# Loading the edge indices of a graph kernel: order of the first loads, and how the edge pairs are stored

## The chip, the cores and the metric

The kernel runs on one core of a Trainium2 chip. The metric is the device time of one execution in microseconds; several executions are timed and their median is given. The profile is of one further execution, with its own time. Engines are called TensorE (PE in the profile; PEld is its weight load), VectorE (DVE), ScalarE (ACT), GpSimd (POOL) and SyncE (SP). SyncE, ScalarE and GpSimd each issue DMA transfers from a queue of their own; in the profile q1 holds SyncE's transfers, q10 ScalarE's and q0 GpSimd's.

## What is computed

There are 6250 nodes with 64 features and 206,250 directed edges, sorted by their destination `dst`; each node has a self-loop among them. Four graph layers follow one another, each on the layer norm of its input and each added to it:

```python
edge_index = jnp.stack([src, dst])
h = relu(layernorm(x)); x = x + L0(h, edge_index, W3, b3, W4, b4)
h = relu(layernorm(x)); x = x + L1(h, edge_index)
h = relu(layernorm(x)); x = x + L2(h, edge_attr_64, src, dst, ...)
h = relu(layernorm(x)); x = x + L3(edge_index, h)
```

L0 is two normalised graph convolutions with a linear map behind each. L1 is one normalised sum over neighbours. L2 puts every edge's attributes through a small MLP, gates the gathered source node with the result, and takes the root of the mean of squares over each node's edges. L3 is three normalised sums over neighbours, averaged with its input. All but L2 are products of the same 6250 by 6250 matrix of edge counts with node features.

## The kernel before

Nodes are padded to 6272, in 49 blocks (`NB`) of 128 (`P`). The kernel builds the matrix of edge counts once, in 8-bit floats, and keeps it in DRAM as `A`. It multiplies with it in every layer but L2. `fast` is the path that runs; `general` follows only if the edges break an assumption of `fast`.

The part that the change touches is the very beginning of `fast`, which prepares the matrix:

- X, the node features, is loaded by ScalarE's queue (L752). `dst` is loaded as `dst_i` by SyncE (L762) and `src` as `src_i` by ScalarE (L764). Both are 128 rows of `K1` = 1616 indices, 206,848 (`EP`) with padding.
- `look` (L767) is every 101st `dst`, times 49. It is stored to DRAM as `looks` (L770), and later read back onto all partitions as `near`, 128 rows of 2048 numbers (L800).
- VectorE makes of every edge a pair of floats, `dst * 49 + (src >> 7)` and `src & 127` (L772 to L777), and SyncE stores these 128 rows of 12,928 bytes to DRAM as `pairs` (L778). Then one row `none`, filled with a large number, is stored over everything from edge 206,250 (`E`) on (L781). The tail of the pair store and this filler cover the same places.
- For 25 columns (`GC`) of 128 two-node groups, VectorE compares `near` with each group's first key and counts (L804), which gives `begin_i`, the approximate position of each group's edges (L807 to L809, in three pieces). The pools that follow (`rpool`, `opool`, `wpool`) reuse the memory of the index tiles and of `near`.
- GpSimd gathers `near2`, 101 pairs from that position on (L872; the profile calls it `near`), VectorE counts again for the exact position, and GpSimd gathers `run`, 128 pairs from there (L881). This happens 25 times each. The gathers read `pairs` as a whole tensor, so they come after every store into it.
- From the runs, `key` is made through TensorE's transposes. `build` compares it with running numbers, which gives one-hot tiles `lo` and `hd` (L852), and their product is 32 columns of counts (L861). ScalarE writes them to a `strip` of 448 columns (L865). SyncE stores each of the 14 strips to `A` (L997).
- The node degrees come from the keys of all runs, over `degs` and `by_block` (L921, L924). They are needed for the normalised features `U3`, with which the first convolution starts (L748).

The layer norm of X (L694 to L703, in 7 groups) and the turning of W3 and W4 (loads L822 and L824, TensorE L833 and L836, copies L834 and L837) also lie in this stretch.

The order of instructions on each engine is the planner's. It works from the program's order and from times that it assumes, except in blocks that are marked as ordered by hand; the beginning is not marked. [...] A tile's memory is given out again when the accesses to it are finished.

Of the kernel before, what the change touches and what calls it, by code (L numbers as in the profile page):

```python
# [8 lines left out]
F32 = mybir.dt.float32  # L9
BF16 = mybir.dt.bfloat16  # L10
FP16 = mybir.dt.float16
I32 = mybir.dt.int32
AF = mybir.ActivationFunctionType
OP = mybir.AluOpType
AX = mybir.AxisListType

P = 128
N = 6250
D = 64
NB = 49  # L20
# [4 lines left out]
E = 206250  # L25
J = 8
G = -(-E // (P * J))
EP = G * P * J
# [556 lines left out]
K1 = EP // P  # L585
LOOK = 101
NS = K1 // LOOK * P
# [29 lines left out]
def fast(ctx, tc, bad, x, src, dst, edge_attr, W3, b3, W4, b4, w1, b1, w2, b2, Bw, Bb, Cw, Cb,  # L617
         pAw, pAb, pBw, pBb, out):

    nc = tc.nc  # L620
# [11 lines left out]
    pairs = dram.tile([EP + 512, 2], F32, name="pairs")  # L632
    looks = dram.tile([NS], F32, name="looks")
# [115 lines left out]
                             start=(i < 2), stop=(i >= 3 * n - 2))  # L749

    X = node.tile([P, NB, D], F32, name="X")
    nc.scalar.dma_start(X, x.rearrange("(b p) f -> p b f", p=P))  # L752
    apart = ctx.enter_context(ExitStack())
    early = ExitStack()
    early_pool = early.enter_context(tc.tile_pool(name="early_pool", bufs=1, reuse_waits="tile"))
    with ExitStack() as ph:

        ipool = ph.enter_context(tc.tile_pool(name="ipool", bufs=1, reuse_waits="tile"))
        with ExitStack() as first:
            dpool = first.enter_context(tc.tile_pool(name="dpool", bufs=1, reuse_waits="tile"))  # L760
            dst_i = dpool.tile([P, K1], I32, name="dst_i")
            nc.sync.dma_start(dst_i, dst.rearrange("(p k) -> p k", p=P))  # L762
            src_i = dpool.tile([P, K1], I32, name="src_i")
            nc.scalar.dma_start(src_i, src.rearrange("(p k) -> p k", p=P))  # L764

            look = dpool.tile([P, NS // P], F32, name="look")
            nc.vector.tensor_scalar(  # L767
                look, dst_i.rearrange("p (i l) -> p i l", l=LOOK)[:, :, 0], float(NB), None,
                op0=OP.mult)
            nc.sync.dma_start(looks.rearrange("(p i) -> p i", p=P), look)  # L770
            hi = dpool.tile([P, K1], I32, name="hi")
            nc.vector.tensor_scalar(hi, src_i, 7, None, op0=OP.logical_shift_right)  # L772
            nc.vector.tensor_scalar(src_i, src_i, P - 1, None, op0=OP.bitwise_and)
            pair = dpool.tile([P, K1, 2], F32, name="pair")
            nc.vector.scalar_tensor_tensor(pair[:, :, 0], dst_i, float(NB), hi,
                                           op0=OP.mult, op1=OP.add)
            nc.vector.tensor_copy(pair[:, :, 1], src_i)  # L777
            nc.sync.dma_start(pairs[:EP, :].rearrange("(p k) t -> p k t", p=P), pair)  # L778
            none = dpool.tile([1, 2 * (EP + 512 - E)], F32, name="none")
            nc.vector.memset(none, float(2 ** 22))  # L780
            nc.sync.dma_start(pairs[E:, :].rearrange("(o e) t -> o (e t)", o=1), none)  # L781

        start_of = ipool.tile([P, GC], F32, name="start_of")
        nc.gpsimd.iota(start_of, pattern=[[2 * NB * P, GC]], base=0, channel_multiplier=2 * NB,
# [9 lines left out]
        begin_i = ipool.tile([P, GC], I32, name="begin_i")  # L794
        exact_i = ipool.tile([P, GC], I32, name="exact_i")
        junk = ipool.tile([P, P], F32, name="junk")
        looked = ExitStack()
        npool = looked.enter_context(tc.tile_pool(name="npool", bufs=1, reuse_waits="tile"))
        near = npool.tile([P, NS], F32, name="near")
        nc.sync.dma_start(near, looks.partition_broadcast(P))  # L800
        for c0, c1 in ((0, 3), (3, 10), (10, GC)):
            for c in range(c0, c1):
                w = min(max(int(c * 2 * P * E / N / LOOK) - 22, 0), NS - SW)
# [4 lines left out]
                                    op0=OP.mult, op1=OP.max)  # L808
# [21 lines left out]
        with ExitStack() as ps:  # L830
            psum = ps.enter_context(tc.tile_pool(name="ps0", bufs=1, space=PSUM, reuse_waits="tile"))
            p = psum.tile([P, SG, P], F32, name="p_a", bufs=2)
            nc.tensor.transpose(p[:D, 0, :], W3_sb, ident)  # L833
            nc.vector.tensor_copy(W3T, p[:D, 0, :])  # L834
            p = psum.tile([P, SG, P], F32, name="p_a", bufs=2)
# [34 lines left out]
            for c in range(GC):  # L870
# [6 lines left out]
                                        op0=OP.is_lt, op1=OP.add, accum_out=n)  # L877
                nc.vector.tensor_add(exact_i[:, c:c + 1], begin[:, c:c + 1], n)
            for c in range(GC):
# [6 lines left out]
                                        op0=OP.subtract)  # L886
                nc.scalar.activation(digits[:, 1, :], run[:, :, 1], AF.Copy)
                p = psum.tile([P, 1024], BF16, name="p_dig")
# [6 lines left out]
                if c % 9 == 8 or c == GC - 1:  # L895
                    c0 = c // 9 * 9
                    p = psum.tile([P, 512], F32, name="p_node")
# [19 lines left out]
            p = psum.tile([P, 512], F32, name="p_node")  # L917
# [7 lines left out]
            p = psum.tile([P, 512], F32, name="p_node")  # L925
# [571 lines left out]
    with ExitStack() as ph:  # L1497
# [5 lines left out]
        for layer in range(3):  # L1503
# [25 lines left out]
            else:  # L1529
                for s in range(CS):  # L1530
                    if s % 2 == 0:
                        whole = apool.tile([P, CB, W], COUNT, name="piece")
                        nc.sync.dma_start(whole, A[s // 2][:, blocks(NC - 1), :])
                    t = whole[:, :, s % 2 * CW:(s % 2 + 1) * CW]
                    p = psum.tile([P, 512], F32, name="p_sum", bufs=2)
# [9 lines left out]
def gnn_kernel(tc, *args):  # L1545
    nc = tc.nc
    with tc.tile_pool(name="verdict", bufs=1) as verdict:
        bad = verdict.tile([1, 1], I32, name="bad")
        fast(tc, bad, *args)
        n = nc.values_load(bad[0:1, 0:1], min_val=0, max_val=2 ** 30)  # L1550
        with tc.If(n > 0):
            general(tc, *args)
# [31 lines left out]
```

## Time and profile before

| | us |
|---|---|
| median of 3 runs | 3608.37 (3608.08 to 3612.73) |
| profiled execution, its own time | 3611.97 |
| its span, first to last instruction | 3610.2 |
| first indirect gather of `pairs` (L872) | starts 48.11 |
| first convolution (L748) | starts 156.9 |
| first product with `A` from DRAM (L1026) | starts 579.0 |
| gathers of the edge layer (L1354) | 1041.9 to 3125.3 |
| last matmul (L1026) | starts 3601.5 |

Over the span TensorE is busy 84%, VectorE 54%, GpSimd 46% and ScalarE 34%; the mean granted TensorE clock is 0.904. Times in the profile run from the span's start. A line of a timeline gives start, length, engine, line, operation, output and input, and in brackets the engine's idle time before it and what ended that. A DMA-issuing instruction is shown on its queue (SPq, ACTq) with the time of the issue; the transfer itself comes later. The DMA view counts packets for each queue[...].

### The profile page before, as it was taken

Reading aid. Unit: us, or ns where it says so; the run is one execution under the profiler, and the core shown is the slowest. Engines: PE = TensorE matmul, PEld = TensorE weight load, DVE = VectorE, ACT = ScalarE, POOL = GpSimd, SP = SyncE. Lnnn points to the kernel's source line nnn. Section 1 sums busy time; section 2 is a strip of 40 time slices with the busy share of each in tenths; the row PEclk is TensorE's granted clock in tenths of the full one; section 3 lists DMA queues with packets and bytes.
Section 4 is the critical chain, followed back from the end, with each engine's and each line's share of the span. In section 5 each row is a group of like instructions: output and inputs, shape, how many; then the busy total and the mean of one; then the engine's idle time right before and its main releaser. Section 6 shows DMA issues by size and latency. Waiting matters only on the chain.

```text
span 3610.2 us, 59581 instructions
## 1 busy us (share of the span) xinstructions
PE 3039.4 (84%) x24393; PEld 2141.2 (59%) x24393; DVE 1954.2 (54%) x3899; ACT 1239.3 (34%) x2024; POOL 1665.0 (46%) x1889
## 2 busy tenths in 40 slices
PE   1699999999977777878878887878887888799999
PEld 0466667999954444444444444444454444489998
DVE  6899993532235546556555655655655565531111
ACT  1577772000023434434333443434433444210000
POOL 4200001000037777777777777777777777400000
PEclk9699999999988888889889888888988888799999
DMA  3233335565532223223323232322332322256664
GB/s 107 64 91 95 95 95 189 188 205 183 178 101 80 77 53 84 71 70 97 86 68 97 70 85 79 88 68 76 91 88 70 94 70 68 81 166 194 196 206 143
DMA packets 229312, 388.76 MB, mean 108 GB/s; under 512 B 137573, under 2 KB 139743, under 8 KB 228771
## 3 DMA queue, kind: packets, MB, share of 16 engines
q1 hardware_dynamic: 170420, 321.51, 28.3%
q0 software_dynamic: 55104, 60.65, 8.3%
q8 instruction: 193, 3.16, 0.4%
q10 hardware_dynamic: 3504, 2.70, 0.3%
q14 instruction: 91, 0.75, 0.1%
HBM read 340.47 MB, written 44.24 MB: 107 GB/s over the span
## 4 chain that ended last, share of the span: by engine, by line
POOL 35%; PE 35%; issue 14%; DMA 9%; DVE 5%; ACT 1%; POOLq 0%; DVEq 0%; SPq 0%; ACTq 0%
POOL v L1354 35%; PE p_acc L1026 21%; PE p_sum L748 7%; DMA v<-Vp_dram,src_g 7%; PE p_a L861 4%; DMA near<-pairs,begin_i 1%; PE p_node L739 1%; DMA piece<-A 1%; DVE lo L852 0%; DMA run<-pairs,exact_i 0%; PE p_acc L1023 0%; PE p_node L970 0%; PE p_bc L1380 0%; DMA X<-in_x 0%; PE p_node L975 0%
## 5 line engine op out<-in xcount | busy, mean ns | idle before, releaser
L1354 POOL DMA_INDIRECT v<-Vp_dram,src_g x1616 | 1592.1, 985 | 859.9 <-issue 828.6
L1026 PE MATMUL p_acc<-U,piece 128*128 128x192 bf16 x9604 | 817.7, 246 | 5.0 <-DMA piece<-A 5.0
L1026 PEld LDWEIGHTS <-piece 128*128 128x128 fp8e4 x9604 | 798.9, 98 | 17.0 <-DMA piece<-A 5.2
L1380 PE MATMUL p_bc<-BC,h 128*128 128x256 f32 x1616 | 585.8, 496 | 0.0
L1389 DVE TENSOR_TENSOR m<-gate,v 128x512 f32<-128x512 f32 x202 | 140.3, 694 | 762.5 <-DMA v<-Vp_dram,src_g 627.7
L1380 PEld LDWEIGHTS p_bc<-BC,h 128*128 128x128 f32 x1616 | 341.2, 234 | 154.7 <-issue 116.2
L1396 ACT ACTIVATE m<-m 128x512 bf16<-128x512 f32 x202 | 127.2, 630 | 821.9 <-DVE m L1391 821.9
L748 PEld LDWEIGHTS <-U 128*64 128x64 bf16 x4116 | 231.1, 112 | 215.4 <-issue 68.3
L1036 DVE TENSOR_REDUCE zg<-p_acc 128x128 f32<-128x384 f32 x112 | 56.3, 507 | 537.4 <-PE p_acc L1026 536.9
L865 ACT ACTIVATE strip<-p_a 128x784 fp8e4<-128x784 f32 x392 | 302.3, 820 | 112.6 <-PE p_a L861 112.0
L1376 PE MATMUL p_bc<-BC_b,ones 3*128 3x512 bf16 x404 | 180.9, 448 | 167.3 <-DVE m L1390 167.2
L1260 PE MATMUL p_sum<-ident_b,piece 128*128 128x128 bf16 x1372 | 154.9, 238 | 183.7 <-DVE junk L1266 183.4
L1260 PEld LDWEIGHTS <-piece 128*128 128x128 fp8e4 x1372 | 117.7, 107 | 318.8 <-issue 301.2
L1376 PEld LDWEIGHTS <-ones 3*128 3x128 bf16 x404 | 37.5, 93 | 439.4 <-DVE m L1390 235.3
L1366 PE MATMUL p<-h,w_d 128*128 128x512 f32 x404 | 253.5, 713 | 38.6 <-ACT h L1370 38.6
L748 PE MATMUL p_sum<-piece,U 128*64 128x448 fp8e4 x2058 | 238.1, 374 | 27.0 <-DVE junk L1266 18.7
L1370 ACT ACTIVATE h<-p,b_c 128x512 f32<-128x512 f32 x404 | 255.8, 684 | 12.9 <-PE p L1366 12.6
L1266 DVE SCALAR_TENSOR_TENSOR junk<-p_sum,there 128x512 bf16<-128x512 f32 (+1 forms) x392 | 242.1, 618 | 27.3 <-PE p_sum L1260 18.7
L748 PE MATMUL p_sum<-strip,U 128*64 128x448 fp8e4 x2058 | 242.0, 359 | 2.5 <-ACT U L711 1.4
L852 DVE TENSOR_TENSOR lo<-count,key 128x2048 bf16<-128x2048 bf16 x196 | 239.6, 1222 | 0.0
L861 PEld LDWEIGHTS <-lo 128*128 128x128 bf16 x3136 | 164.7, 103 | 98.6 <-DVE lo L852 75.8
L861 PE MATMUL p_a<-hd,lo 128*128 128x98 bf16 x3136 | 195.1, 217 | 32.6 <-DVE lo L852 31.1
(198 smaller groups left out, 3308.5 us busy)
## 6 DMA issues: line engine op xcount, KB each, us to landing
piece<-A SPq DMA_DIRECT2D x249, 784.0 KB, 4.3
e<-in_edge_attr SPq DMA_DIRECT2D x202, 256.0 KB, 2.7
A<-strip SPq DMA_DIRECT2D x14, 2744.0 KB, 13.1
v<-Vp_dram,src_g POOLq DMA_INDIRECT x1616
there<-A SPq DMA_DIRECT2D x28, 784.0 KB
pairs<-pair SPq DMA_DIRECT2D x1, 1616.0 KB, 5.3
Vp_dram<-v SPq DMA_DIRECT2D x7, 224.0 KB
out<-X SPq DMA_DIRECT2D x6, 224.0 KB
```

Of the source, the lines that this page charges most:

```text
L748: nc.tensor.matmul(p[half * D:(half + 1) * D, :w], U3[:, b, k, :], at_block, start=(i < 2), stop=(i >= 3 * n - 2))
L852: nc.vector.tensor_tensor(t, of.unsqueeze(1).to_broadcast(t.shape), key[:, k, at:at + GB].rearrange("p (h j) -> p h j", j=GQ) .unsqueeze(2 ...
L861: nc.tensor.matmul(p[:, j, :2 * NB], lo[:, g // GQ, :, g % GQ], hd[:, g // GQ, :, g % GQ], start=True, stop=True)
L865: nc.scalar.activation(strips[s][:, :, col:col + 2 * SG].rearrange("p b (j l) -> p b j l", l=2), p[:, :, :2 * NB].rearrange("p j (b l) -> ...
L1026: nc.tensor.matmul(p[d // 2][:, d % 2 * 3 * D:(d % 2 + 1) * 3 * D], t[:, b, d * P:(d + 1) * P], U3[:, k * CB + b, :, :].rearrange("p t f - ...
L1260: nc.tensor.matmul(p[:, a - a0, :], held["here", i, k][:, a, b * P:(b + 1) * P], ident_b, start=True, stop=True)
L1266: nc.vector.scalar_tensor_tensor(junk[:, :(a1 - a0) * P], p[:, :a1 - a0, :].rearrange("p a q -> p (a q)"), 15.5, of_there, op0=OP.min, op1 ...
L1354: nc.gpsimd.indirect_dma_start(out=v[:, j, :], out_offset=None, in_=Vp_dram[:, :], in_offset=bass.IndirectOffsetOnAxis(ap=src_g[:, g, j:j ...
L1366: nc.tensor.matmul(of[g][p], w, of[g].pop(x), start=True, stop=True)
L1370: nc.scalar.activation(of[g][t], of[g].pop(p), **how)
L1376: nc.tensor.matmul(p_bc[:, 4 * b:4 * b + 4].rearrange("p j o f -> p (j o f)"), ones, BC_b, start=True, stop=False)
L1380: nc.tensor.matmul(p_bc[:, 2 * q:2 * q + 2].rearrange("p j o f -> p (j o f)"), h2[:, q * P:(q + 1) * P], BC, start=False, stop=(k == 1))
```

## The change

- `src_i` is loaded by SyncE behind `dst_i`.
- `near` gets its memory before the index tiles, in a stack that is closed after the comparisons, and is read directly behind the store of `looks`. The index tiles stay allocated as long.
- X's load is traced behind these, still on ScalarE's queue.
- `none` is filled at the start.
- The pair store is cut in two: `whole` = E // K1 = 127 rows, and of the last row the pairs that belong to real edges, 1018. The filler is stored behind them and overlaps neither.

```diff
     X = node.tile([P, NB, D], F32, name="X")
-    nc.scalar.dma_start(X, x.rearrange("(b p) f -> p b f", p=P))
...
-        with ExitStack() as first:
-            dpool = first.enter_context(tc.tile_pool(name="dpool", bufs=1, reuse_waits="tile"))
-            dst_i = dpool.tile([P, K1], I32, name="dst_i")
-            nc.sync.dma_start(dst_i, dst.rearrange("(p k) -> p k", p=P))
-            src_i = dpool.tile([P, K1], I32, name="src_i")
-            nc.scalar.dma_start(src_i, src.rearrange("(p k) -> p k", p=P))
...
-            nc.sync.dma_start(pairs[:EP, :].rearrange("(p k) t -> p k t", p=P), pair)
-            none = dpool.tile([1, 2 * (EP + 512 - E)], F32, name="none")
-            nc.vector.memset(none, float(2 ** 22))
-            nc.sync.dma_start(pairs[E:, :].rearrange("(o e) t -> o (e t)", o=1), none)
+        looked = ExitStack()
+        npool = looked.enter_context(tc.tile_pool(name="npool", bufs=1, reuse_waits="tile"))
+        near = npool.tile([P, NS], F32, name="near")
+        dpool = looked.enter_context(tc.tile_pool(name="dpool", bufs=1, reuse_waits="tile"))
+        none = dpool.tile([1, 2 * (EP + 512 - E)], F32, name="none")
+        nc.vector.memset(none, float(2 ** 22))
+        dst_i = dpool.tile([P, K1], I32, name="dst_i")
+        nc.sync.dma_start(dst_i, dst.rearrange("(p k) -> p k", p=P))
+        src_i = dpool.tile([P, K1], I32, name="src_i")
+        nc.sync.dma_start(src_i, src.rearrange("(p k) -> p k", p=P))
...
+        nc.sync.dma_start(looks.rearrange("(p i) -> p i", p=P), look)
+        nc.sync.dma_start(near, looks.partition_broadcast(P))
+        nc.scalar.dma_start(X, x.rearrange("(b p) f -> p b f", p=P))
...
+        whole = E // K1
+        nc.sync.dma_start(pairs[:whole * K1, :].rearrange("(p k) t -> p k t", k=K1),
+                          pair[:whole])
+        nc.sync.dma_start(pairs[whole * K1:E, :].rearrange("(o k) t -> o k t", o=1),
+                          pair[whole:whole + 1, :E - whole * K1, :])
+        nc.sync.dma_start(pairs[E:, :].rearrange("(o e) t -> o (e t)", o=1), none)
...
-        looked = ExitStack()
-        npool = looked.enter_context(tc.tile_pool(name="npool", bufs=1, reuse_waits="tile"))
-        near = npool.tile([P, NS], F32, name="near")
-        nc.sync.dma_start(near, looks.partition_broadcast(P))
```

The pair arithmetic itself, left out above, is only moved to the left by one level.

More of the change, by code (lines that the diff above doesn't have):

```diff
@@ L758, in fast @@
         ipool = ph.enter_context(tc.tile_pool(name="ipool", bufs=1, reuse_waits="tile"))
-        with ExitStack() as first:
-            dpool = first.enter_context(tc.tile_pool(name="dpool", bufs=1, reuse_waits="tile"))
-            dst_i = dpool.tile([P, K1], I32, name="dst_i")
-            nc.sync.dma_start(dst_i, dst.rearrange("(p k) -> p k", p=P))
-            src_i = dpool.tile([P, K1], I32, name="src_i")
-            nc.scalar.dma_start(src_i, src.rearrange("(p k) -> p k", p=P))
[L766 to L778, printed above, removed]
-            none = dpool.tile([1, 2 * (EP + 512 - E)], F32, name="none")
-            nc.vector.memset(none, float(2 ** 22))
-            nc.sync.dma_start(pairs[E:, :].rearrange("(o e) t -> o (e t)", o=1), none)
@@ new lines, in fast @@
+        src_i = dpool.tile([P, K1], I32, name="src_i")
+        nc.sync.dma_start(src_i, src.rearrange("(p k) -> p k", p=P))
+        look = dpool.tile([P, NS // P], F32, name="look")
+        nc.vector.tensor_scalar(
+            look, dst_i.rearrange("p (i l) -> p i l", l=LOOK)[:, :, 0], float(NB), None,
+            op0=OP.mult)
+        nc.sync.dma_start(looks.rearrange("(p i) -> p i", p=P), look)
+        nc.sync.dma_start(near, looks.partition_broadcast(P))
+        nc.scalar.dma_start(X, x.rearrange("(b p) f -> p b f", p=P))
@@ new lines, in fast @@
+        hi = dpool.tile([P, K1], I32, name="hi")
+        nc.vector.tensor_scalar(hi, src_i, 7, None, op0=OP.logical_shift_right)
+        nc.vector.tensor_scalar(src_i, src_i, P - 1, None, op0=OP.bitwise_and)
+        pair = dpool.tile([P, K1, 2], F32, name="pair")
+        nc.vector.scalar_tensor_tensor(pair[:, :, 0], dst_i, float(NB), hi,
+                                       op0=OP.mult, op1=OP.add)
+        nc.vector.tensor_copy(pair[:, :, 1], src_i)
+        whole = E // K1
+        nc.sync.dma_start(pairs[:whole * K1, :].rearrange("(p k) t -> p k t", k=K1),
+                          pair[:whole])
```

## Prediction

> **What bounds the kernel now, at the place that is changed.** I read the chain of waits of the first 60 us first, because every line of the diff runs before the first indirect gather.
>
> ```profile
> 0.86 11.79 DMA X<-in_x
> 12.68 1.15 DVE m L694 x2
> ...
> 17.98 1.75 DVE pair L775
> ...
> 47.84 0.19 DVE begin L807
> 48.11 1.12 POOL near L872
> ```
>
> The columns are start, length and what ran. X arrives, VectorE then works without a gap (layer norm, pairs, layer norm, the 25 comparisons of L804), and GpSimd's first gather from `pairs` starts when L804 and L807 are through. The gather's wait, from GpSimd's timeline:
>
> ```profile
> 48.11 1.12 POOL L872 DMA_INDIRECT near<-pairs,begin_i  x1 [43.52 <-DVE begin L807]
> ```
>
> It names VectorE, so `pairs` was ready earlier. SyncE's timeline says by how much:
>
> ```profile
> 0.81 0.41 SPq L762 DMA_DIRECT2D dst_i<-in_dst  x1
> 5.78 0.33 SPq L770 DMA_DIRECT2D looks<-look  x1
> 20.67 0.32 SPq L778 DMA_DIRECT2D pairs<-pair  x1
> 25.96 0.29 SPq L781 DMA_DIRECT2D pairs<-none  x1
> 26.35 0.34 SPq L800 DMA_DIRECT2D near<-looks  x1
> ```
>
> The filler overlaps the pairs, so it waits 5.29 us for them, and `near` is queued behind both. `pairs` is complete at about 27.5 us: it has 20 us to spare before 48.1. This margin decides the case.
>
> Next, does a later first gather cost its full delay? The table of windows from there to the first convolution (columns: window, length, busy time of PE, weight loads, VectorE, ScalarE, GpSimd, then clock, DMA share, GB/s):
>
> ```profile
> 57.00:101.00 44.00, 13.64 (x150) 10.53 (x151) 28.31 (x102) 12.46 (x23) 31.61 (x31) 1.00 0.30 84
> 101.00:121.00 20.00, 12.26 (x139) 10.34 (x138) 18.14 (x32) 13.41 (x23) 7.72 (x8) 0.67 0.17 47
> 121.00:144.00 23.00, 11.72 (x140) 9.16 (x140) 15.71 (x34) 8.11 (x16) 4.46 (x5) 0.50 0.56 152
> 144.00:157.00 13.00, 8.55 (x89) 6.96 (x86) 12.75 (x21) 10.13 (x16) 0.00 (x0) 0.50 0.02 5
> ```
>
> All of it works on gathered pairs: GpSimd's gathers lead until 101, VectorE's one-hot tiles after that. The degrees, and with them the first convolution at 156.9 us, need every gather. Nothing there could run ahead of the first one; the layer norm is done by 38 us already. From 157 on, TensorE and, in the edge layer, GpSimd carry the chain to the end. So a delay of the first gather moves the end by the same amount.
>
> [...]counting packets on SyncE's queue, q1, in four windows of the DMA view (packets, MB, share of 16 engines); in order, 20 to 26, 144 to 145.3, 145.3 to 148 and 3604.7 to 3609 us.
>
> ```profile
> q1 hardware_dynamic: 144, 1.65, 66.2%
> ...
> q1 hardware_dynamic: 30, 0.03, 6.5%
> ...
> q1 hardware_dynamic: 56, 0.03, 3.2%
> ...
> q1 hardware_dynamic: 892, 0.22, 22.2%
> ```
>
> The pair store has 128 rows and 144 packets: 16 completions. `degs<-by_col` has 25 rows and 30 packets: 5. `by_block<-degs` has 49 and 56: 7. The two last stores of `out` have 768 + 106 rows and 892 packets: 18, that is 16 + 2. So 25, 49 and 106 rows got 5, 7 and 2 engines[...], with no transfer cut up to use more. [...]
>
> [...]`looks<-look` is issued on SyncE at 5.78 us, but from 6 to 10 us ScalarE's X fills the engines (share 1.12), and the 64-byte rows move only when X is nearly in.
>
> **The change, part by part.**
>
> (1) *src on SyncE behind dst; X traced later.* X's load waits for nothing and nothing precedes it on ScalarE's queue, so I expect it at about 0.9 us still. Two places for src: ahead of X's bytes, it takes what dst took (dst is in at 5.58) and lands near 9 us; behind them, it lands near 15 us as now (L772 starts at 15.54). The pair arithmetic on VectorE is 1.00 + 0.99 + 1.83 + 1.00 = 4.8 us. The pair store is then issued at about 14 or 20 us, against 20.67; I take 17, with 14 to 21 as bounds.
>
> (2) *`near` has its own memory and is issued directly behind `looks`.* Its 1 MB took about 5 us (26.35 to 31); it is now in by some 14 to 20 us. L804's 25 comparisons at a pitch of 0.39 us (10 us) can finish by 30 to 38 us. By itself this would bring the first gather forward by 10 to 18 us.
>
> (3) *The filler no longer overlaps*: its 4.9 us wait on SyncE goes, and `near` no longer stands behind it. Worth nothing by itself, as the 20 us of margin cover it. The memset moves forward on an idle VectorE: nothing.
>
> (4) *The pair store is cut.* E is 206,250 and K1 is 1616, so `whole` is 127. The large part has 127 rows of 12,928 B, 1.642 MB; a second part has one row of 8,144 B, the filler is one row of 8,880 B. [...]all three run on **one engine**. The rate of one engine, from the table of windows while the 128-row store ran:
>
> ```profile
> 22.00:24.00 2.00, 0.00 (x0) 0.00 (x0) 2.00 (x6) 0.30 (x1) 0.00 (x0) 1.00 1.01 420
> ```
>
> 420 GB/s on 16 engines at share 1.01 is 26 GB/s each. [...]I take the measured 26: 1.642 MB / 26 = 63.1 us. The two small pieces follow on that engine: 17 KB, 0.65 us. The fixed part is 5.29 less 1.655 MB / 420 (3.94), or 1.35 us. `near` and X may still be sharing that engine at the start: a sixteenth of 1.05 MB at 26 is 2.5 us. I take 1 of 0 to 4.
>
> The sum: 17 + 1.35 + 63.1 + 0.65 + 1 is **83 us for the first gather**, against 48.1. Bounds: [...]21 + 1.35 + 65 + 0.7 + 2 is 90 (65 us being a rate of 25.2). Parts 1 to 3 are then hidden: L804 is done long before, and GpSimd waits for the store in its place. What is queued behind the waiting gather on GpSimd is the other 49 gathers, and for these wait VectorE, TensorE and ScalarE. On SyncE nothing is due until the strip store (121 us before). The delay is 83 - 48.1, **+35 us** (+28 to +42).
>
> Of the profiled execution (span 3610.2, time 3611.97) that makes a span of 3645. The execution lies 3.6 us above the median, 3608.37, so I forecast 3608.4 + 35, about 3643. A measurement of this kernel can tell some 0.2%, 7 us, from no change.
>
> **Rivals.**
>
> *A. The store spreads and the reordering pays (faster).* If the 127 rows went to all engines, `pairs` would be complete near 23 us and L804's end would decide, at 30 to 38 us: 10 to 18 us gained. Some layer norm (7 groups of about 3.3 us) would then run beside the gathers, where VectorE idles 15.7 of 44 us; I charge 0 to 6 us for that and arrive at -12: 3596. The turning point: the store must be in by 48 us, so 1.64 MB in about 28 us, 59 GB/s, three engines. For it speaks only that no large transfer of 127 rows is in the trace; against it stand the counts of 5, 7 and 2. Chance 6%; 2% for an outcome near zero.
>
> *B. The late store holds up VectorE too (slower still).* The first pool tiles reuse the memory of the index tiles. If W3's and W4's load (32.15 us before) had to wait for the pair tile, VectorE's copies L834 and L837 would stand in its queue until 85 us, and what follows them (L804's 10 us, a group or two of layer norm) would precede the first gather: 95 us, +47, 3655. For it: before, too, this load comes after the store. Against: the index tiles now lie in front of `pair` and are free much earlier. Chance 12%.
>
> *C. The change doesn't do what it says.* X stays first and src comes behind it: pair store at 20 to 21 us, first gather at 86, +38: 3646. This has the same sign, and lies inside the main case.
>
> **How the numbers follow.** Main case with C: 80%, at +28 to +42. B 12%, A 6%, none 2%. The range runs from 3632 (+24: the low bound, less 4 us for a different interleaving behind the first gather) to 3656 (+48, which takes in B). Below it lie A and the small rest. Slower 92%, within 0.2% 2%, faster 6%.
>
> **What would show it.** In the changed profile: q1 has 128 packets (127 + 1) for the large part, the DMA share stands at about 0.06 with 26 GB/s from some 20 to 82 us, the first gather's wait ends on a DMA of `pairs`, not on L807, and L804 has been done for over 40 us. The first convolution starts near 192 us, and the stages after it keep their lengths. It is wrong if the store lands within 10 us of its issue, if the first gather waits for VectorE, or if the stage from first gather to first convolution (108.8 us) gets shorter by more than 5 us.

## The result, and the profile after

| | before | changed |
|---|---|---|
| median, us | 3609.76 (4 runs, one more than above) | 3643.09 (3642.70 to 3648.81, 4 runs) |
| ratio | | 1.0099, 95% interval 1.0087 to 1.0111 |
| profiled execution, its own time | 3611.97 | 3642.88 |
| its span | 3610.2 | 3641.1 |
| first indirect gather of `pairs` | 48.11 | 82.10 |
| first convolution | 156.9 | 191.6 |
| last convolution of a strip starts | 573.4 | 608.0 |

The changed kernel is 33.3 us slower by the medians. Lines behind the change lie 3 further down: L872 is now L875, L804 is L807.

The chain of waits of the first 90 us of the changed kernel (start, length, what ran):

```profile
4.58 76.35 another core or an unknown queue
...
82.10 1.12 POOL near L875
```

Before, X's load and then VectorE filled this chain. Now, behind GpSimd's own preparations of the first 4.6 us, no compute engine is in it: for 76 us it hangs on something that this view cannot name. GpSimd's timeline names it, a store into `pairs`:

```profile
82.10 1.12 POOL L875 DMA_INDIRECT near<-pairs,begin_i  x1 [77.52 <-DMA pairs<-pair]
```

SyncE's timeline shows when the parts of that store were issued:

```profile
1.27 0.41 SPq L767 DMA_DIRECT2D src_i<-in_src  x1
5.46 0.33 SPq L773 DMA_DIRECT2D looks<-look  x1
5.84 0.33 SPq L788 DMA_DIRECT2D pairs<-none  x1
13.29 0.34 SPq L774 DMA_DIRECT2D near<-looks  x1
13.67 0.29 SPq L784 DMA_DIRECT2D pairs<-pair  x1
21.71 22.52 SPq L786 DMA_DIRECT2D pairs<-pair  x1
```

The planner put the filler early (5.84). The 127 rows are issued at 13.67 us, 7 us sooner than the 128 rows before. The remaining row at 21.71 takes 22.5 us to issue at all. The table of windows of the changed kernel (columns as in the prediction; the last two are the DMA share and GB/s) shows the transfer:

```profile
13.00:19.00 6.00, 0.00 (x0) 0.00 (x0) 2.95 (x7) 0.00 (x0) 0.00 (x0) 1.00 0.70 200
19.00:20.00 1.00, 0.00 (x0) 0.00 (x0) 0.71 (x3) 0.00 (x0) 0.00 (x0) 1.00 0.06 26
...
79.00:80.00 1.00, 0.00 (x0) 0.00 (x0) 0.00 (x0) 0.00 (x0) 0.00 (x0) 1.00 0.06 26
80.00:80.50 0.50, 0.00 (x0) 0.00 (x0) 0.00 (x0) 0.00 (x0) 0.00 (x0) 1.00 0.04 16
80.50:81.00 0.50, 0.00 (x0) 0.00 (x0) 0.00 (x0) 0.00 (x0) 0.00 (x0) 1.00 0.00 0
```

A share of 0.06 is one engine of sixteen (1/16 is 0.0625). It stands there, at 26 to 27 GB/s, from 19 us until about 80.5 (from 20 to 30 us small loads of ScalarE add to it: 0.11, 36 GB/s): 1.642 MB in 61.4 us. The DMA view from 30 to 80 us gives the same for SyncE's queue (packets, MB, share):

```profile
q1 hardware_dynamic: 104, 1.34, 6.3%
```

104 rows of 12,928 B in 50 us are 0.48 us each. The packet counts agree. A transfer shows small packets besides its rows: of the 144 of the 128-row store before, 16 are under 512 B. From 13 to 82 us the changed kernel's queue has 274 packets, which are 128 + 16 for `near`, 127 + 1 for the large part and 1 + 1 for the last row. The number of these small packets goes with the share: 16 with 1.01 in the store before, one with 0.06 here, two with 0.14 in run 4. So I read them as completions, one for each engine used. The stage behind, first gather to first convolution, in the same kind of table:

```profile
82.10:191.60 109.50, 46.36 (x513) 37.21 (x513) 79.14 (x205) 44.33 (x78) 51.82 (x50) 0.77 0.29 81
```

It takes 109.5 us; in the kernel before it took 156.9 - 48.1, or 108.8. The delay passes through almost unchanged.

### The profile page after: what moved, and what is told of

Same layout as the page of the kernel before. It is cut to its first block, busy times and chain, and to the rows that moved or that the text cites. A ratio compares the mean times of both kernels' runs of the same rounds, so it can differ in the third digit from the quotient of the medians.

```text
span 3641.1 us, 59581 instructions
## 1 busy us (share of the span) xinstructions
PE 3037.0 (83%) x24393; PEld 2130.9 (59%) x24393; DVE 1953.2 (54%) x3899; ACT 1240.2 (34%) x2024; POOL 1662.7 (46%) x1889
## 4 chain that ended last, share of the span: by engine, by line
PE 35%; POOL 35%; issue 14%; DMA 7%; DVE 4%; another core or an unknown queue 2%; ACT 1%; POOLq 0%; DVEq 0%; SPq 0%; ACTq 0%
POOL v L1357 35%; PE p_acc L1029 20%; PE p_sum L748 7%; DMA v<-Vp_dram,src_g 6%; PE p_a L864 4%; PE p_node L739 1%; DMA near<-pairs,begin_i 1%; PE p_bc L1383 1%; DMA piece<-A 1%; DVE lo L855 0%; DMA run<-pairs,exact_i 0%; PE p_acc L1026 0%; PE p_node L973 0%; PE p_node L978 0%
```

## Experiments

The first four runs and the three numbered 9 to 11 fell on two chips that granted TensorE less clock (about 0.85, against 0.90 to 0.91 on the others): there the kernel before takes 4123 and 4165 us instead of 3608, and the intervals are wider. Each ratio is to the kernel before on the same chip. Where a kernel was executed only once, its time stands in place of the ratio. The starts of the first gather and the first convolution come from each run's trace, in us.

| run | first gather | first convolution | ratio to before (95%), or one time in us |
|---|---|---|---|
| 1 split alone | 101.22 | 216.1 | 1.0108 (1.0042 to 1.0173) |
| 2 rows 112 and 15 | 38.54 | 155.2 | 1.0002 (0.9975 to 1.0029) |
| 3 whole store | 38.12 | 155.9 | 0.9996 (0.9970 to 1.0021) |
| 4 rows 122 and 5 | 50.71 | 168.4 | 4155.47 |
| 5 before again | 48.30 | 158.3 | 3614.11 |
| 6 changed again | 82.27 | 191.6 | 3643.95 |
| 7 X behind near | 29.84 | 150.6 | 0.9989 (0.9982 to 0.9996) |
| 8 row on GpSimd | 81.89 | 191.1 | 3646.95 |
| 9 rows 112 and 15 | 38.38 | 155.6 | 0.9983 (0.9958 to 1.0009) |
| 10 X last | 27.51 | 153.5 | 0.9984 (0.9960 to 1.0008) |
| 11 norm behind | 27.20 | 148.1 | 0.9990 (0.9963 to 1.0017) |
| 12 rows 112 and 15 | 38.36 | 149.7 | 0.9982 (0.9974 to 0.9989) |

**1. The split alone, in the kernel before.**

```diff
-            nc.sync.dma_start(pairs[:EP, :].rearrange("(p k) t -> p k t", p=P), pair)
+            whole = E // K1
+            nc.sync.dma_start(pairs[:whole * K1, :].rearrange("(p k) t -> p k t", k=K1),
+                              pair[:whole])
+            nc.sync.dma_start(pairs[whole * K1:E, :].rearrange("(o k) t -> o k t", o=1),
+                              pair[whole:whole + 1, :E - whole * K1, :])
```

> The kernel before with one edit: the pair store is cut into 127 rows and the rest of row 127, everything else as it was. One-engine theory: the store is issued near 20.7 us and takes 127 x 0.484 us = 61.5 us and 1 to 3 us more; the first gather starts at 84 to 88 us against 48.1, and the time rises by 35 to 40 us, as much as with the whole change or a little more, since the store starts 7 us later. Rival, the delay comes from the new order of the loads or from the memory of near and the index tiles: this kernel stays within 5 us of the kernel before.

The first gather comes 53 us later than before, more than expected. The extra comes from VectorE's comparisons, which end only at 100.9 us here. These lines of SyncE's, ScalarE's and VectorE's timelines say why:

```profile
20.83 0.25 SPq L779 DMA_DIRECT2D pairs<-pair  x1
21.12 27.12 SPq L781 DMA_DIRECT2D pairs<-pair  x1
48.34 1.75 SPq L804 DMA_DIRECT2D near<-looks  x1
...
84.39 0.34 ACTq L826 DMA_DIRECT2D W_sb<-in_L_gnn_W  x1
...
85.62 0.20 DVE L702 RECIPROCAL v<-v 128x7 f32<-128x7 f32 x1 [52.87 <-ACT v L701]
```

ScalarE stands from 28.0 us until W3's load can be issued at 84.39, when the last bytes of the store have just moved. VectorE's layer norm waits 52.9 us for ScalarE behind it, and the 25 comparisons come after that, from 89.8 us on; they do not wait for `near`. The profile does not name what W3's load waited for; its time fits the wait for memory that the prediction has as rival B. (`near` is late too: its issue stands behind the split store until 48.34, and of its 128 rows 8 move only after 83.9 us. But it was not the last.) Then 11 us of comparisons follow where the changed kernel has none left. So the split by itself makes the whole loss and more; the new order of the loads and of the memory in the changed kernel takes part of it back. The rival is out. The lower clock of this chip (0.858 in the profiled execution) changes nothing in the store: from 55 to 82 us 56 rows move, again 0.48 us each.

**2, 9 and 12. The changed kernel with 112 and 15 rows.**

```diff
-        nc.sync.dma_start(pairs[:whole * K1, :].rearrange("(p k) t -> p k t", k=K1),
-                          pair[:whole])
+        for r0, r1 in ((0, 112), (112, whole)):
+            nc.sync.dma_start(pairs[r0 * K1:r1 * K1, :].rearrange("(p k) t -> p k t", k=K1),
+                              pair[r0:r1])
```

> The whole change, but the 127 rows are stored as 112 and 15. One-engine theory with its rule of divisors: 16 and 15 engines, both landed within 7 us of the issue near 13.7 us, W3 and W4 arrive early, and VectorE's comparisons decide again: the first gather starts at 34 to 40 us (in the changed kernel they ended at 51, of which 13.5 us were waits for W3 and W4), so the time is 8 to 14 us under the kernel before. Rival, the number of rows does not matter and the store is slow because of its place in the program or its last row: the first gather stays near 82 us, time +33.

> The whole change with 112 and 15 rows again, since it ran on a chip that granted TensorE less clock. One-engine theory: first gather at 38 to 39 us as there. Of the 9.6 us that the first gather comes earlier, layer norm behind it gives some back. If the 6 us stall of TensorE belongs to that chip, the first convolution is at 148 to 151 us here and the time 4 to 9 us under the kernel before; if it belongs to the kernel, it is at 154 to 156 us and the time within 4 us.

> The whole change with 112 and 15 rows once more: both runs of it so far fell on chips where the kernel before takes 4120 to 4165 us, not 3608. One-engine theory: first gather at 38 to 39 us on any chip. On a chip where the kernel before takes 3608 us: if the stalls of TensorE seen on the other chips belong to those chips, the first convolution is at 148 to 152 us and the time 3 to 9 us under the kernel before; if they belong to this kernel's order, it is at 154 to 156 us again and the time within 3 us of it.

The same 127 rows go out as two transfers, and the first gather starts at 38.4 to 38.5 us in all three runs, 44 us sooner than in the changed kernel. It waits for VectorE again, as this line of run 12's GpSimd timeline shows (L811 is the end of the comparisons):

```profile
38.36 1.12 POOL L876 DMA_INDIRECT near<-pairs,begin_i  x1 [33.78 <-DVE begin L811]
```

The small packets agree again. From 13 to 26 us SyncE's queue has 304 packets in each of the three runs: 128 + 16 for `near`, 112 + 16 and 15 + 15 for the two parts, 1 + 1 for the last row. The only edit was the cut of the rows, so the number of rows decides, not the place of the store or the last row. On the chip where the kernel before takes 3608.44 us, run 12 takes 3601.39: 7 us faster than before, and 42 us faster than the changed kernel's 3643.09, a median taken on another chip. On the two slower chips the first convolution came at 155 us and no gain can be told from the intervals, so the 8 to 14 us expected of run 2 were not met, and run 9's first convolution, at 155.6, is the one that its expectation had put down to the kernel. The same kernel's stage behind the first gather took 117 us there and 111 here. Before the products of L865, TensorE stands still there for no cause that the trace shows: between 30 and 220 us, 11.3 us in run 2 (the longest 5.9) and 6.3 us in run 9 (4.7). Run 12 has no such wait, so they go with the chips and not with the order of this kernel.

**3. One store of 128 rows with the filler over its tail, everything else as changed.**

```diff
-        whole = E // K1
...
+        nc.sync.dma_start(pairs[:EP, :].rearrange("(p k) t -> p k t", p=P), pair)
```

> The whole change, but the pairs are stored in one piece of 128 rows as before, with the filler stored over its tail. One-engine theory: 16 engines; the filler waits about 5 us for the store, so all of pairs is in by 22 to 24 us, still ahead of VectorE's comparisons; same time as with 112 and 15 rows within 3 us. That is, the overlap itself costs nothing. Rival, the overlap is what the kernel before paid for: 4 to 5 us slower than with 112 and 15 rows.

First gather 38.12 us, beside 38.54 in run 2 on the same chip. SyncE waits from 14.4 to 24.2 us before it issues the filler, longer than the 5 us expected, but that is still 14 us before the comparisons end. So the overlap that the change removes cost the first gather nothing; the intervals of the two ratios are too wide for the 3 us expected of the time.

**4. Two engines: 122 and 5 rows.** The edit is that of run 2 with 122 for 112.

> The whole change, but the 127 rows are stored as 122 (2 x 61) and 5. One-engine theory: 122 rows take two engines, 61 x 0.484 = 29.5 us and some contention with near and W3; 5 rows take five engines. Pairs are in at 45 to 49 us, and the first gather starts at 45 to 50 us, by the store or by comparisons that W3 held up: time within 5 us of the kernel before. Rival, any cut store is slow: first gather near 82 us. Rival, the last row alone is slow: first gather near 82 us too.

```profile
30.00:40.00 10.00, 0.00 (x0) 0.00 (x0) 7.82 (x33) 0.30 (x1) 0.00 (x0) 1.00 0.14 56
```

In run 4's table of windows the share is 0.14 at 56 GB/s, twice what the changed kernel shows; 0.125 would be two engines. The first gather waits for the store until 50.71 us. From 13 to 52 us SyncE's queue has 280 packets: 128 + 16, 122 + 2, 5 + 5 and 1 + 1. Both rivals are out (they expected 82), and in all these transfers the number of small packets goes with the divisors of the row count: 128 and 112 rows have 16, 15 have 15, 5 have 5, 122 (2 x 61) have 2, and 127, a prime, have one. Whether the time is within 5 us of the kernel before, as expected, its single 4155.47 cannot tell: the kernel before ranges from 4097.80 to 4163.27 on this chip.

**5 and 6. Both kernels again, unchanged, on one chip.**

> The kernel before, unchanged, for a profile on the same chip as the experiments, since TensorE's clock was granted less there. First theory for the gain that got lost (first gather 9.6 us earlier with 112 and 15 rows, first convolution only 1.7 us earlier): the stage from first gather to first convolution is lengthened by layer norm that moved behind the first gather; then this kernel keeps its 108.8 us here. Second theory: the stage is longer on this chip, whatever the kernel (a stall of TensorE of about 6 us near the eighth run); then it shows 114 to 118 us here.

> The changed kernel, unchanged, for a profile on the same chip. One-engine theory: the first gather at 82 us as before[...]. Stage from first gather to first convolution: 109 to 111 us if its length belongs to the kernel, 114 to 118 us if it belongs to the chip.

The first gathers repeat within 0.2 us, the stages are 110.0 and 109.3 us. The two single times differ by 29.8 us. This chip granted the usual clock, so the two runs could not decide between the theories named; run 12 did.

**7. X's load really later.** In the changed kernel ScalarE still issues X at 0.86 us, since nothing stands before it on that queue. Here it is issued by SyncE and held behind the read of `near`; pairs in 112 and 15 rows.

```diff
-        nc.sync.dma_start(near, looks.partition_broadcast(P))
-        nc.scalar.dma_start(X, x.rearrange("(b p) f -> p b f", p=P))
+        behind = nc.sync.dma_start(near, looks.partition_broadcast(P))
+        with tc.issue_after(behind.ins):
+            nc.sync.dma_start(X, x.rearrange("(b p) f -> p b f", p=P))
```

> The kernel with 112 and 15 rows, and X's load is issued by SyncE and held behind the read of near, so that X really comes later. Theory that X's bytes hold up looks (5.5 us issued, over 6 us until it moves): looks and near now come before X, near is in at 12 to 14 us, the 25 comparisons end at 23 to 25 us, X and the pair store are in by about 25 us, and the first gather starts at 24 to 27 us, 12 to 14 us earlier than with 112 and 15 rows alone. First convolution 8 to 12 us earlier, if layer norm fits beside the gathers; 3 to 6 if it does not. Rival, X does not matter[...]: first gather stays at 35 to 39 us.

The comparisons run from 16.8 to 26.7 us instead of 19.7 to 38.1 in run 12, and the first gather starts at 29.84. That is some 3 us later than expected; by its packets the pair store, issued at 13.57 us, stood behind the bytes of X, issued at 12.44 on the same queue. X did hold up `looks`: from its issue to that of `near`, which waits for it, 2.8 us pass here (9.10 to 11.90) and 7.8 in the changed kernel. That lets the comparisons start 2.9 us earlier. The larger part of the gain is that X is not there yet, so that no layer norm lies among the comparisons: they take 10 us instead of 18. But the first convolution, at 150.6, is no earlier than in run 12, so the 3 to 12 us expected of it were not met. GpSimd's timeline of run 7 shows where 12 us went:

```profile
32.53 0.95 POOL L877 DMA_INDIRECT near<-pairs,begin_i  x1 [0.30 <-issue]
45.75 1.09 POOL L877 DMA_INDIRECT near<-pairs,begin_i  x1 [12.27 <-DVE junk L881]
```

After three gathers GpSimd waits for VectorE's first lookup (L881). The planner had put most of layer norm in front of it. Against the kernel before this is still 0.1% faster.

**8. The last row from GpSimd's queue.**

```diff
-        nc.sync.dma_start(pairs[whole * K1:E, :].rearrange("(o k) t -> o k t", o=1),
+        nc.gpsimd.dma_start(pairs[whole * K1:E, :].rearrange("(o k) t -> o k t", o=1),
```

> The changed kernel, but the last row's 1018 pairs are stored from GpSimd's queue, so that SyncE's queue holds only the 127 rows. The issue of that row kept SyncE's queue busy for 22.5 us in the changed kernel, and W3, issued at 24.2 us on ScalarE, was in only at 42.8. If W3 was late because SyncE's issue blocked the making of transfers: it is in within 4 us now, and VectorE does not stand still for 11.7 us. If it was late because its rows share the one engine with the large rows: still late, 10 us or more. In both cases the first gather stays at 80 to 83 us, since the 127 rows decide it.

Here SyncE's queue is free after 13.9 us. W3 is issued at 21.8 us, and TensorE still waits for it until 42.9, as the list of waits of this run says:

```profile
PE p_a L836 <- DMA W_sb<-in_L_gnn_W: 42.9, 1, 42.9
...
DVE W3T L837 <- PE p_a L836: 15.4, 1, 15.4
```

So the long issue is not what made W3 late. That its rows share the one engine with the large rows fits the DMA view: from 28.5 to 42.5 us, in this run and in the changed kernel alike, SyncE's queue moves 29 packets and ScalarE's 29. That is one small packet for each large row, at the pace of the large rows: 14 us / 29 is 0.48 us. The first gather stays at 81.9.

**10 and 11. X last, and layer norm behind the lookups.** Both have 112 and 15 rows. In run 10 X is issued by SyncE and held behind the last store of pairs. In run 11, in addition:

```diff
+            with tc.issue_after(found):
+                for c in range(NC):
+                    normed(H0[:, blocks(c), :], X[:, blocks(c), :])
```

stands behind both gather loops, where `found` is the third lookup's last instruction; the earlier loop of layer norm is gone.

> 112 and 15 rows, and X's load is issued by SyncE and held behind the stores of pairs. With X behind near the pair store stood behind X's bytes and landed near 28 us, and the first gather began at 29.8 while the comparisons were over at 26.9; now the first gather starts at 26 to 28 us. In the planner's order, layer norm stands in one block before VectorE's seventh and eighth lookups, and GpSimd must wait there: theory of layer norm in front, the stage from first gather to first convolution is again 118 to 124 us, and the first convolution at 145 to 150. Rival, the long stage with X behind near came from X's late arrival itself: the stage is then longer than 124 us.

> As the kernel with X last, but layer norm is traced behind both gather loops and held behind the third lookup, so that in VectorE's order all lookups and one-hot tiles of the first strip come first, as in the kernel before. Theory of layer norm in front: GpSimd no longer waits for a block of layer norm; first gather 26 to 28 us, the stage to the first convolution 109 to 120 us (the 23 us of layer norm now lie among the last keys, where VectorE is nearly full), first convolution at 136 to 146 us, time 12 to 20 us under the kernel before. Rival, VectorE's sum of work decides and not its order: first convolution as with X last, within 3 us.

The first gathers came at 27.5 and 27.2 us, as expected. The stages behind took 126.0 and 120.9 us, on the chip where run 9's stage is 6 us longer than run 12's (117.2 and 111.3). Run 10's 126.0 lies on the side of its rival (over 124), and its first convolution at 153.5 is later than either expected; with 6 us that may be the chip's in it the run does not decide. The expectation for run 11, 12 to 20 us under the kernel before, failed: the first convolution came at 148.1, but the last one started at 576.2, beside 572.4 in run 9 on the same chip. Layer norm and the one-hot tiles of the next strips all need VectorE, and the likely reading, which no run tests, is that moving the norm only moved the lack: 400 of TensorE's matmuls lie in this stage of run 11, 513 in run 9's. How much of the possible 20 us an order by hand could keep is left open; neither run is distinguishable from the kernel before by its interval.

## Why the prediction was right, point by point

- **One engine for 127 rows.** Right. The share was 0.06 at 26 GB/s, and runs 2 and 4 show 16 and 15, and two engines for other row counts. Before the result this was my estimate from the counts of the trace before: 128, 25, 49 and 106 rows had 16, 5, 7 and 2 small packets, each time the largest divisor up to 16, and for the prime 127 that is 1. The 63.1 us of the sum were 61.4. The low end of the delay, +28, was my estimate; no run shows the rate behind it.
- **Issue of the store at 17 us.** It was 13.67: src came ahead of X's bytes (VectorE's first step on it, L777, starts at 7.81), the better of the two cases. This term was 3.3 us too long.
- **1.35 us of fixed cost and 1 us of sharing.** From issue to the first bytes it took 5.3 us, because `near` had been issued 0.4 us before on the same queue and moved first (from 13.6 to 18 us SyncE's queue moves 1.03 MB; `near` is 1.05). With the term above, 17 + 1.35 + 1 = 19.35 stands against a measured 19.0: two errors that cancelled, which is luck.
- **0.65 us for the small pieces.** The filler was out early and only one row followed. Instead, some 1.6 us passed from the last bytes to the gather (80.5 to 82.1). The 1.35 us, taken from a whole store's time, were to hold this end too, and did not. The sum was 83, the gather came at 82.1.
- **What hides parts 1 to 3.** Right, but by less than I said. The comparisons were to be over 40 us before the gather; they ended at 50.6, 31 us before, because VectorE stood 11.7 and 1.8 us for W3 and W4 (L837, L840). This is rival B's effect by another cause: W3's load did not wait for memory, it was issued at 24.15 us, and it came late (42.9), by my reading because it shared the engine. It ended early enough to cost nothing. Where the order of the memory is the old one, in run 1, the wait that B describes does seem to come (W3 issued at 84.39), and there it cost time.
- **The delay passes to the end.** 34.0 us at the first gather, 34.7 at the first convolution, 34.6 at the last one, 30.9 in the span, 33.3 in the medians. The span's figure is smaller because the edge layer, which was not touched, took 2079.8 us instead of 2083.4. In runs 5 and 6 it took 2081.9 and 2082.2, so this is the scatter of single executions and not a difference between the kernels.
- **Rival A** would have been the outcome with 112 and 15 rows: -7 us (run 12) where I had written -12. The first gather at 38.4 is just past the late end of my 30 to 38, since layer norm lies between the comparisons, and the stage behind grew by 2.5 us.
- **Rival C** was half right: X did stay first on its queue, but src was not held up by it (L777 starts at 7.81); `looks` was, issued at 5.46 and moved between 10 and 13 us.

## What to carry to other kernels

Before cutting a transfer, factor its row count: here 128 rows and 127 rows differ by 0.8% in bytes, and the transfer took 61.4 us where 128 rows at the measured 420 GB/s took an estimated 3.9; 112 + 15 rows held up the first gather no more than 128 did (38.54 us in run 2, 38.12 in run 3). Read such a store in the DMA share: 0.06 means one engine of the sixteen. And before paying to bring a transfer forward, look at what is queued on the engine that consumes it; here 10 to 20 us at the start became 7 at most. Layer norm moved in behind the first gather, which is seen in run 7; in runs 10 and 11 it stays the likely cause.

## What the runs showed of the hardware that I had not expected

- A small load on another queue came late while the large rows moved: W3's 32 KB were issued at 24.15 us, and TensorE could use them at 42.86 in the changed kernel; before, they were issued at 32.15 and used at 34.1. From 28.5 to 42.5 us, with the share at 0.06, SyncE's queue moved 29 large rows and ScalarE's 29 small packets, which I read as the two taking turns on that engine. In run 12 VectorE didn't wait for W3 at all.
- The issue itself can be long: one row of 8 KB, issued behind the 127 rows, kept SyncE's queue for 22.5 us in the changed kernel and for 27.1 us in run 1. There `near`, the next on that queue, was issued at 48.34 us, 0.1 us after it ended. No run shows what the issue itself waits for.
- X's load held up a small transfer of another queue: `looks`, 8 KB, was issued on SyncE at 5.46 us, and `near`, which waits for it, could be issued only at 13.29. From 6 to 10 us ScalarE's queue moved 797 packets with 0.82 MB, at a share of 1.06 to 1.10; the rows of `looks` moved from 10 to 13. With X held back, in run 7, the two issues are at 9.10 and 11.90.
